# A decoder layer on one core: packing the query weights after the first keys, turning x1 before the cross value halves, and another order in the last section and the scatters

## The chip, the cores and the metric

The kernel runs on one core of a Trainium2 chip. The metric is the device time of one execution in microseconds (us), as the median of several runs. All times below are in us from the start of the span of one profiled execution, unless it is said otherwise. The engines are named as in the profile: PE (TensorE matmul), PEld (its weight load), DVE (VectorE), ACT (ScalarE), POOL (GpSimd) and SP (SyncE, which here issues DMAs). PE's clock can be granted at less than full speed; the profile shows it as a share, 1.00 being full.

## The reference

One decoder layer in float32 over 32 samples of 256 tokens with 256 channels: causal self-attention in a latent space (16 heads, 72 latent channels shared by keys and values), cross-attention to 120 context rows (16 heads of 64), and a mixture of 16 experts in which every expert takes its 32 best tokens of each sample, plus one shared feed-forward. A residual add and a layernorm follow each of the three blocks. Cut to what matters:

```python
kv = x @ latent_w + latent_b                        # (32, 256, 72)
q = einsum('btc,hcl->bhtl', x, Wd_w) + Wd_b         # 16 heads
attn = softmax(causal(q @ kv^T / sqrt(16)))
x1 = layernorm(x + concat_heads(attn @ kv) @ out_w + out_b)

w = softmax((x1 @ Wq * 64**-0.5) @ (ctx @ Wk)^T)    # 16 heads of 64, 120 rows
x2 = layernorm(x1 + (w @ (ctx @ Wv)) @ Wo)

scores = softmax(x2 @ gate_w^T)                     # 16 experts
topk_w, topk_idx = top_k(scores per expert, 32)     # of each sample's 256 tokens
eo = (gelu(xe @ Wg^T) * (xe @ Wu^T)) @ Wd^T * topk_w
out = layernorm(x2 + scatter_add(eo) + shared_expert(x2))
```

## The kernel before

**The rounds.** Attention runs sample by sample. `attention_round(n)` (L778) does the self-attention of sample n, the cross-attention of sample n-1 and the end of the cross-attention of sample n-2 (`cross_out`, `turn_x2`). For n = 1 to 31 the order of PE's instructions is the written one (`manual_schedule` for PE); in round 0 and ahead of it SP's order is the written one too. The other engines' orders are made by a scheduler; what stands in `urgent()` gets a higher priority there. A round takes about 75.5 us. In seven rounds (n = 6, 10, ... 30) the gate's work of four earlier samples is done besides (`routed(n)`, which calls `route` and `score`).

**The first part of a round.** `first_section(n)` (L742) ends with `latent_out(n-1)` (L486): po, the add with x (the r1 add, L496, DVE) and layernorm 1, which makes x1. `layernorm` (L141 to L161) takes its statistics on DVE (L149, L150), rstd on POOL (L152), and the result on DVE again (L154). Then `first_section_rest(n)` (L760) follows with `cross_out(n-2)` (L615: po, the r2 add L625, layernorm 2), `cross_values` (L521: pvx, one half of the heads per call, copied out by ACT), `turn_x1` (L500: transposes into px1T, which `transposed` at L163 has DVE copy into x1T, L172), the second half of `cross_values`, and `cross_queries` (pqx), which reads x1T. `cross_scores` (L555) computes pL and its softmax; POOL does the division, xsm_x (L417). `cross_turn` (L576) transposes that (pxT), `cross_weigh` (L593) applies it to the values (pc). Self-attention has the same steps: `scores` (pS, sm), `turn` (pT), `weigh` (L446, pz), `weigh_rest` (L469, pzr).

**The start.** The block at L838 loads x and the weights, turns x (`turn_x` L297: pxT, xT; POOL then adds out_b, `outb`, to x), computes the keys (`keys` L304: pk) and then queries. `first_weights` (L221) issues the loads of the query weights and packs them from their staging tile ow_sb into wd_sb: two copies at L242 and pack 0 at L236 on DVE, packs 1 to 3 on POOL, and the scalings of wdbs on DVE.

**The last section and the experts.** After round 31 stand `first_section(32)` and a block in which PE's and POOL's orders are both the written ones. There the rest of sample 31's cross-attention alternates with the feed-forward work: `feed_forward()` (L998) is a generator that yields between small stretches of work, and `fill(k)` advances it by k stretches. Its units are (twice) 16 experts and 8 shared ones, each of two samples. An expert's `load` (from L880) has SP load three weight matrices and POOL gather four blocks of 128 rows (xe, L889); `turn` transposes them (px, L898, into xeT); `gated` makes hT (pg and pu, eight stretches); `down` (L910) makes pd in two halves (one stretch each), scales them into a tile eo, and after both scatters four blocks back into acc (L929). The first two stretches are unit 0's `load`, and unit 1's `load` with unit 0's `turn`.

Of the kernel before, what the change touches and what calls it, by code (L numbers as in the profile page):

```python
# [20 lines left out]
F32 = mybir.dt.float32  # L21
# [5 lines left out]
P = 128  # L27
# [5 lines left out]
def decoder_kernel(  # L33
# [140 lines left out]
    def project(acc, pairs):  # L174

        n = len(pairs)
        for i, (lhsT, rhs) in enumerate(pairs):
            nc.tensor.matmul(acc, lhsT, rhs, start=(i == 0), stop=(i == n - 1))  # L178
# [42 lines left out]
    def first_weights():  # L221


        raw = ow_sb.rearrange("p a b -> p (a b)").rearrange("p (c n) -> p c n", c=DC)
        nc.sync.dma_start(out=lat_sb, in_=latent_w.rearrange("(c p) l -> p c l", p=P))
        nc.sync.dma_start(out=raw, in_=wd_w.rearrange("(c p) n -> p c n", p=P))
        nc.scalar.dma_start(out=latb, in_=latent_b.unsqueeze(1))
        nc.scalar.dma_start(
            out=wdbs[:, ZC - 1 : ZC], in_=wd_b[LM:, :].rearrange("l h -> (l h)").unsqueeze(1)
        )  # L230
        nc.scalar.dma_start(out=wdb_sb, in_=wd_b)
        by_head = raw.rearrange("p c (h l) -> p c h l", l=L)

        def pack(copy, g):
            at = slice(2 * g * P, 2 * (g + 1) * P)
            copy(  # L236
                wd_sb[:, :, at].rearrange("p c (h l) -> p c h l", l=LM),
                by_head[:, :, g * HG : (g + 1) * HG, 0:LM],
            )

        for d in range(DC):
            nc.vector.tensor_copy(  # L242
                wd_sb[:, d, H * LM :].rearrange("p (l h) -> p l h", h=H),
                by_head[:, d, :, LM:].rearrange("p h l -> p l h"),
            )

        nc.vector.tensor_scalar(
            wdbs[:, ZC - 1 : ZC], wdbs[:, ZC - 1 : ZC], QSCALE, None, ALU.mult
        )
        pack(nc.vector.tensor_copy, 0)  # L250
        for odd in range(2):
            nc.vector.tensor_scalar(
                wdbs[odd * LM : (odd + 1) * LM, 0 : H // 2],
                wdb_sb[0:LM, :].rearrange("l (c two) -> l c two", two=2)[:, :, odd],
                QSCALE,
                None,
                ALU.mult,
            )
        for g in range(1, NG):
            pack(nc.gpsimd.tensor_copy, g)  # L260
        nc.sync.dma_start(out=outb, in_=out_b.partition_broadcast(P))

    def load_weights(pairs):
        for t, w in pairs:
# [39 lines left out]
    def keys(s):  # L304

        st = states[s]
        pk = bank("r", [L, T], f"pk_{st['nm']}")
        project(pk, [(lat_sb[:, c, :], st["xT"][:, c, :]) for c in range(DC)])
        st["kT"] = sp.tile([L, T], F32, tag="kT", name=f"kT_{st['nm']}")
        with urgent():  # L310
            nc.scalar.activation(st["kT"], pk, AF.Identity, bias=latb)
# [420 lines left out]
    def run(step, s, *args):  # L732
        if 0 <= s < B:
            step(s, *args)
# [7 lines left out]
    def first_section(n):  # L742
# [14 lines left out]
        run(cross_weigh, n - 2, 4)  # L757
        run(latent_out, n - 1)

    def first_section_rest(n):  # L760
        if n:
            run(load, n + 1)
            run(load_context, n + 1)
        run(cross_out, n - 2)
        run(cross_values, n - 1, 0)
        run(turn_x1, n - 1)
        run(cross_values, n - 1, 1)
        if routed(n):
            score((n - 3) // BQ)
        run(cross_queries, n - 1, 0, 0)  # L770
        run(cross_queries, n - 1, 0, 2)
        run(cross_queries, n - 1, 4, 0)
        run(cross_scores, n - 1, 0, 0)
        run(cross_queries, n - 1, 4, 2)
# [63 lines left out]
    with tc.manual_schedule(engines={mybir.EngineType.PE, mybir.EngineType.SP}):  # L838
        load(0)
        first_weights()  # L840
        load_context(0)
        turn_x(0)
        keys(0)
        query_rest(0)
        queries(0, 0)
        values(0)
        load(1)
        load_context(1)
        load_weights([(wk_sb, wk)])
        attention_round(0)  # L850
    with tc.manual_schedule(engines={mybir.EngineType.PE}):
        for n in range(1, B):
            attention_round(n)
        first_section(B)
    self_pools.close()


# [9 lines left out]
    class Expert:  # L867
# [39 lines left out]
        def begin(self):  # L907
            pass

        def down(self):  # L910
            eo = fp.tile([P, NBK, C], F32, tag="eo", bufs=2, name=f"eo_{self.nm}")
            for k0 in range(0, NBK, 2):
                pd = bank("r", [P, 2, C], f"pd_{self.nm}_{k0}")
                for k in range(2):
                    tok = slice((k0 + k) * P, (k0 + k + 1) * P)
                    project(
                        pd[:, k, :], [(self.hT[:, j, tok], self.wd[:, j, :]) for j in range(FC)]
                    )
                for k in range(2):
                    score = self.xe[:, k0 + k, C + self.e : C + self.e + 1]  # L920
                    if k % 2:
                        nc.scalar.activation(eo[:, k0 + k, :], pd[:, k, :], AF.Copy, scale=score)
                    else:
                        nc.vector.tensor_scalar(  # L924
                            eo[:, k0 + k, :], pd[:, k, :], score, None, ALU.mult
                        )
                yield
            for k, b in enumerate(self.blocks):
                nc.gpsimd.indirect_dma_start(  # L929
                    out=acc[b],  # L930
                    out_offset=self.rows(b),
                    in_=eo[:, k, :],
                    in_offset=None,
                    compute_op=ALU.add,
                )

    class Shared:
# [24 lines left out]
                nc.sync.dma_start(out=back, in_=rows.rearrange("(t p) d -> p t d", p=P))  # L962
                self.backs.append(back)

        def down(self):
            for i, back in enumerate(self.backs):
                s = 2 * self.pair + i
                po = bank("r", [P, TC, C], f"pfo_{s}")
                for t in range(TC):
                    tok = slice(i * T + t * P, i * T + (t + 1) * P)  # L970
                    project(
                        po[:, t, :], [(self.hT[:, j, tok], self.wd[:, j, :]) for j in range(FC)]
                    )
                rows = out[s].rearrange("(t p) d -> p t d", p=P)
                parts = [slice(0, TC)] if s < B - 1 else [slice(t, t + 1) for t in range(TC)]
                for part in parts:
                    half = back[:, part, :]
                    nc.vector.tensor_tensor(half, po[:, part, :], half, ALU.add)
                    layernorm(fp, half, half, f"3_{s}_{part.start}")
                    nc.sync.dma_start(out=rows[:, part, :], in_=half)  # L980
                yield

    def gated(unit):

# [13 lines left out]
    def feed_forward():  # L998

        units = []  # L1000
        for part in range(B // HB):
            units += [Expert(part, e) for e in range(E)]
            units += [Shared(pair) for pair in range(part * HB // 2, (part + 1) * HB // 2)]
        units[0].load()
        yield
        units[1].load()
        units[0].turn()
        yield
        for u, unit in enumerate(units):
            unit.begin()  # L1010
            yield from gated(unit)
            if u + 1 < len(units):
                units[u + 1].turn()
            yield from unit.down()
            if u + 2 < len(units):
                units[u + 2].load()


    work = feed_forward()
# [5 lines left out]
    last = B - 1  # L1025
    with tc.manual_schedule(engines={mybir.EngineType.PE, mybir.EngineType.Pool}):
        fill(1)
        first_section_rest(B)
        cross_scores(last, 0, 1)
        turn_x2(last - 1)  # L1030
        fill(2)
        for odd in range(2):
            cross_turn(last, 0, 0, odd)
        fill(1)
        cross_scores(last, 4, 0)
        for odd in range(2):
            cross_turn(last, 0, 1, odd)
        fill(2)
        cross_weigh(last, 0)
        cross_scores(last, 4, 1)  # L1040
        for odd in range(2):
            cross_turn(last, 4, 0, odd)
        fill(4)
        for odd in range(2):
            cross_turn(last, 4, 1, odd)
        fill(1)
        cross_weigh(last, 4)
        fill(1)
        cross_out(last)
        fill(3)  # L1050
        turn_x2(last)
        fill(1)
        route(last // BQ)
        fill(1)
        score(last // BQ)
        fill(3)
        select(B // BG - 1)
        fill(8)
        place(B // BG - 1)
        for _ in work:  # L1060
            pass
# [52 lines left out]
```

## Time and profile before

| what | us |
|---|---|
| median of 3 runs | 3493.84 (3493.35 to 3494.77) |
| the profiled execution | 3492.36 |
| its span (first to last instruction) | 3490.2 |
| mean granted PE clock in the span | 0.997 |
| a round without routing, with routing | 75.5, 76.4 |
| one expert unit, once attention is over | 21.5 |

The first rows of the table differ in what they measure: the span leaves out 2.2 us that lie around the instructions, and the profiled execution is one run of its own, 1.5 us below the median. Times that are worked out from the trace belong to the profiled execution.

In the lists below, a line of the timeline gives start, busy time, engine, source line, operation, output and inputs with their shapes, and the count of instructions grouped; in brackets stands the idle time ahead of it and what released it. The time of a group of matmuls includes the modelled drain of its last one, so the next group may start before the end that is shown.

### The profile page before, as it was taken

What the parts mean: (1) busy time and instruction counts of PE and PEld (TensorE: products, weight loads), DVE (VectorE), ACT (ScalarE), POOL (GpSimd) and SP (SyncE); (2) the same over time, 40 slices, a digit from 0 to 9 for tenths busy, and PEclk for the clock granted to TensorE, in tenths of its full rate; (3) what the DMA queues carried; (4) which work ended last, traced back from release to release, by engine and by line L of the source; (5) the groups of instructions that cost most, each with busy time, mean ns of one, the idle gap of its engine ahead of it and who ended that gap; (6) DMA issues with size and microseconds to landing.
All of it is one profiled execution on the core that took longest, in us unless ns stands there. A gap on an engine that the chain in (4) does not pass through costs nothing.

```text
span 3490.2 us, 58138 instructions
## 1 busy us (share of the span) xinstructions
PE 3449.6 (99%) x21468; PEld 2617.0 (75%) x21468; DVE 1632.7 (47%) x3639; ACT 1499.0 (43%) x5456; POOL 1090.3 (31%) x1073
## 2 busy tenths in 40 slices
PE   8999999999999999999999999999999999999999
PEld 6888888888888888888888888887666655666655
DVE  4555555556555555654555565554311233221133
ACT  3555544555554455554455565444311111111111
POOL 2333322233322233332223333222344411444410
PEclk9999999999999999999999999999999999999999
DMA  3000000000000000000000000002455532455421
GB/s 96 14 19 17 17 17 21 22 20 16 17 17 20 24 17 20 17 17 16 20 24 20 17 17 17 16 21 71 95 123 125 138 99 61 110 124 127 104 82 51
DMA packets 144561, 164.42 MB, mean 47 GB/s; under 512 B 31384, under 2 KB 120216, under 8 KB 144280
## 3 DMA queue, kind: packets, MB, share of 16 engines
q1 hardware_dynamic: 119392, 126.09, 12.1%
q0 software_dynamic: 24576, 34.62, 5.7%
q8 instruction: 171, 2.80, 0.3%
q14 instruction: 110, 0.90, 0.1%
q10 hardware_dynamic: 312, 0.01, 0.0%
HBM read 105.61 MB, written 50.86 MB: 45 GB/s over the span
## 4 chain that ended last, share of the span: by engine, by line
PE 94%; DVE 3%; issue 1%; POOL 1%; DMA 1%; SPq 0%; ACT 0%; POOLq 0%; DVEq 0%; ACTq 0%
PE po L178 13%; PE pS L390 10%; PE pq L178 7%; PE pqx L178 7%; PE pd L178 6%; PE pg L178 6%; PE pu L178 6%; PE pz L455 5%; PE pT L435 5%; PE pL L562 4%; PE pxT L585 3%; PE pc L601 3%; PE pkx L178 3%; PE pu_s L178 3%; PE pg_s L178 3%; PE pfo L178 3%
## 5 line engine op out<-in xcount | busy, mean ns | idle before, releaser
L417 POOL TENSOR_TENSOR sm<-sm,rs 128x512 f32<-128x512 f32 x384 | 397.0, 1041 | 361.9 <-DVE rs L416 349.9
L417 POOL TENSOR_TENSOR xsm_x<-xsm_x,rs_x 128x480 f32<-128x480 f32 x256 | 252.7, 987 | 708.9 <-DVE rs_x L416 706.2
L409 ACT ACTIVATE sm<-sm,nmax 128x128 f32<-128x128 f32 (+1 forms) x1024 | 461.4, 466 | 18.4 <-DVE nmax L403 16.8
L409 ACT ACTIVATE xsm_x<-pL,nmax_x 128x120 f32<-128x120 f32 x1024 | 360.5, 376 | 124.7 <-DVE nmax_x L572 124.6
L390 PE MATMUL pS<-kT,qT 72*128 72x128 f32 (+1 forms) x2048 | 380.4, 329 | 3.3 <-DMA qT<-q 2.3
L152 POOL TENSOR_TENSOR rstd<-rstd,mhalf 128x2 f32<-128x2 f32 (+1 forms) x97 | 67.2, 693 | 935.4 <-DVE rstd L151 935.4
L390 PEld LDWEIGHTS pS<-kT,qT 72*128 72x128 f32 x2048 | 294.9, 192 | 21.1 <-ACT sm L409 2.6
L929 POOL DMA_INDIRECT acc<-eo,offs x128 | 201.5, 1574 | 324.5 <-DVE eo L924 295.0
L399 DVE TENSOR_TENSOR sm<-pS,mask 128x512 f32<-128x512 f32 x384 | 261.3, 681 | 70.8 <-PE pS L390 65.0
L178 PE MATMUL pq<-xT,wd_sb 128*128 128x256 f32 x1152 | 278.1, 382 | 0.0
L531 ACT COPY vx<-pvx 120x512 f32<-120x512 f32 x64 | 37.5, 586 | 557.2 <-PE pvx L178 557.2
L403 DVE TENSOR_REDUCE nmax<-sm 128x2 f32<-128x512 f32 (+1 forms) x384 | 258.5, 673 | 2.4
L178 PE MATMUL po<-ow_sb,zT 128*128 128x256 f32 x1152 | 257.2, 382 | 0.0
L995 DVE TENSOR_TENSOR hT<-gl,pu 128x512 f32<-128x512 f32 x128 | 87.9, 688 | 342.6 <-PE pu L178 258.8
L178 PEld LDWEIGHTS po<-ow_sb,zT 128*128 128x128 f32 x1152 | 216.2, 190 | 40.2 <-DVE cxT L613 8.8
L178 PE MATMUL pqx<-x1T,wq_sb 128*128 128x256 f32 x1024 | 238.0, 385 | 6.6 <-DVE x1T L172 6.3
L178 PE MATMUL pg<-xeT,wg 128*128 128x512 f32 x512 | 240.8, 593 | 0.8 <-DVE xeT L905 0.8
L178 PE MATMUL pu<-xeT,wu 128*128 128x512 f32 x512 | 240.6, 592 | 0.0
L178 PEld LDWEIGHTS pqx<-x1T,wq_sb 128*128 128x128 f32 x1024 | 189.4, 190 | 55.6 <-DVE x1T L172 28.3
L178 PEld LDWEIGHTS pq<-xT,wd_sb 128*128 128x128 f32 x1152 | 210.4, 191 | 25.4 <-issue 0.2
L178 PE MATMUL pd<-wd,hT 128*128 128x256 f32 x1024 | 226.6, 379 | 0.0
L178 PE MATMUL po<-wo_sb,cxT 128*128 128x256 f32 x1024 | 226.2, 379 | 0.0
(130 smaller groups left out, 5833.9 us busy)
## 6 DMA issues: line engine op xcount, KB each, us to landing
wg<-in_wg_dram SPq DMA_DIRECT2D x32, 512.0 KB
wu<-in_wu_dram SPq DMA_DIRECT2D x32, 512.0 KB
wd<-in_wd_dram SPq DMA_DIRECT2D x32, 512.0 KB
x<-in_x_dram SPq DMA_DIRECT2D x32, 256.0 KB
qT<-q SPq DMA_DIRECT2D x512, 8.0 KB
rows<-x SPq DMA_DIRECT2D x32, 256.0 KB
acc<-x SPq DMA_DIRECT2D x32, 256.0 KB
x2t<-x2T SPq DMA_DIRECT2D x32, 256.0 KB
```

What stands on the lines that cost most here:

```text
L178: nc.tensor.matmul(acc, lhsT, rhs, start=(i == 0), stop=(i == n - 1))
L390: nc.tensor.matmul(pS[:, a, :], st["qT", g][:, j, t * P : (t + 1) * P], st["kT"][:, 0:width], start=True, stop=True,)
L399: nc.vector.tensor_tensor(sm, pS, m.unsqueeze(1).to_broadcast([P, n, width]), ALU.add)
L403: nc.vector.tensor_reduce(nmax, sm, AX.X, ALU.max, negate=True)
L409: nc.scalar.activation(dst[:, a, :], src[:, a, :], AF.Exp, bias=nmax[:, a : a + 1], accum_out=rs[:, a, :],)
L417: nc.gpsimd.tensor_tensor(dst, dst, rs.to_broadcast([P, n, width]), ALU.mult)
L435: nc.tensor.transpose(pT[:, j, :], block, ident)
L455: nc.tensor.matmul(pz[odd * LM : (odd + 1) * LM, a, k * P :], st["v"][:, k, 0:LM], moving(st, g, 2 * a + odd, k), start=(k == 0), stop=(k ...
L562: nc.tensor.matmul(pLs[odd][:, j, :], st["qxT", c0][rows, j, t * P : (t + 1) * P], st["kxT"][rows, c0 + j, :], start=True, stop=True,)
L585: nc.tensor.transpose(pT[:, j, :], st["xsm", c0, t, odd][:, j, :], ident)
L601: nc.tensor.matmul(pc[odd * DH : (odd + 1) * DH, a, :], st["vx"][:, 2 * (c0 + j0 + a) + odd, :], st["xpt", c0, odd][:, j0 + a, :], start=True,
L929: nc.gpsimd.indirect_dma_start(out=acc[b], out_offset=self.rows(b), in_=eo[:, k, :], in_offset=None, compute_op=ALU.add,)
```

## The change

Four edits.

1. `first_weights` keeps the loads (that of outb among them); the packing goes into a new function `order_weights`, which is called after `keys(0)`.
2. In `first_section_rest`, `turn_x1(n-1)` now stands ahead of both calls of `cross_values`; for n = 1 one half stays where it was.
3. `first_section(32)` is replaced by `last_section()`: the two last weighs of sample 31 are set around its turns, the two cross turns of sample 30 go behind `latent_out`, and sample 30's `cross_weigh` goes to the next block, behind the first `fill(1)`. In that block `turn_x2(30)` and one stretch of feed-forward (the one with unit 1's `load` and unit 0's `turn`) go ahead of `cross_scores(31, 0, 1)`.
4. `down` takes the half as an argument. Each half has its own tile eo (four buffers of half the size instead of two), and scatters its two blocks at once. The `load` of the unit after next is in the same stretch as the second half, ahead of its yield; it was behind it.

```diff
@@ first_weights
         nc.scalar.dma_start(out=wdb_sb, in_=wd_b)
+        nc.sync.dma_start(out=outb, in_=out_b.partition_broadcast(P))
+
+    def order_weights():
+        raw = ow_sb.rearrange("p a b -> p (a b)").rearrange("p (c n) -> p c n", c=DC)
         by_head = raw.rearrange("p c (h l) -> p c h l", l=L)
...
         for g in range(1, NG):
             pack(nc.gpsimd.tensor_copy, g)
-        nc.sync.dma_start(out=outb, in_=out_b.partition_broadcast(P))
@@ the sections
+    def last_section():
+
+        weigh(B - 1, 2)
+        for b in range(3):
+            turn(B - 1, 3, b)
+        weigh(B - 1, 3)
+        weigh_rest(B - 1)
+        latent_out(B - 1)
+        for odd in range(2):
+            cross_turn(B - 2, 4, 1, odd)
+
     def first_section_rest(n):
         if n:
             run(load, n + 1)
             run(load_context, n + 1)
+        if n == 1:
+            cross_values(0, 0)
         run(cross_out, n - 2)
-        run(cross_values, n - 1, 0)
         run(turn_x1, n - 1)
+        if n > 1:
+            run(cross_values, n - 1, 0)
         run(cross_values, n - 1, 1)
@@ the start, and after the rounds
         keys(0)
+        order_weights()
         query_rest(0)
...
-        first_section(B)
+        last_section()
@@ Expert
-        def down(self):
-            eo = fp.tile([P, NBK, C], F32, tag="eo", bufs=2, name=f"eo_{self.nm}")
-            for k0 in range(0, NBK, 2):
...
-                yield
-            for k, b in enumerate(self.blocks):
+        def down(self, k0):
+
+            k0 *= 2
+            eo = fp.tile([P, 2, C], F32, tag="eo", bufs=4, name=f"eo_{self.nm}_{k0}")
...
+            for k in range(2):
+                b = self.blocks[k0 + k]
                 nc.gpsimd.indirect_dma_start(
                     out=acc[b],
@@ feed_forward
-            yield from unit.down()
+            unit.down(0)
+            yield
+            unit.down(1)
             if u + 2 < len(units):
                 units[u + 2].load()
+            yield
@@ the last block
         fill(1)
+        cross_weigh(last - 1, 4)
         first_section_rest(B)
+        turn_x2(last - 1)
+        fill(1)
         cross_scores(last, 0, 1)
-        turn_x2(last - 1)
-        fill(2)
+        fill(1)
```

`Shared.down` is split by samples in the same way.

More of the change, by code (lines that the diff above doesn't have):

```diff
@@ L908, in begin @@
             pass
-        def down(self):
-            eo = fp.tile([P, NBK, C], F32, tag="eo", bufs=2, name=f"eo_{self.nm}")
-            for k0 in range(0, NBK, 2):
[L913 to L926, printed above, removed]
-                yield
-            for k, b in enumerate(self.blocks):
+        def down(self, k0):
+            k0 *= 2
+            eo = fp.tile([P, 2, C], F32, tag="eo", bufs=4, name=f"eo_{self.nm}_{k0}")
+            pd = bank("r", [P, 2, C], f"pd_{self.nm}_{k0}")
+            for k in range(2):
+                tok = slice((k0 + k) * P, (k0 + k + 1) * P)
+                project(pd[:, k, :], [(self.hT[:, j, tok], self.wd[:, j, :]) for j in range(FC)])
+            for k in range(2):
+                score = self.xe[:, k0 + k, C + self.e : C + self.e + 1]
+                if k % 2:
+                    nc.scalar.activation(eo[:, k, :], pd[:, k, :], AF.Copy, scale=score)
+                else:
+                    nc.vector.tensor_scalar(eo[:, k, :], pd[:, k, :], score, None, ALU.mult)
+            for k in range(2):
+                b = self.blocks[k0 + k]
                 nc.gpsimd.indirect_dma_start(
@@ L963, in begin, with down @@
                 self.backs.append(back)
[L965 to L981, printed above, removed]
+        def down(self, i):
+            s = 2 * self.pair + i
+            back = self.backs[i]
+            po = bank("r", [P, TC, C], f"pfo_{s}")
+            for t in range(TC):
+                tok = slice(i * T + t * P, i * T + (t + 1) * P)
+                project(po[:, t, :], [(self.hT[:, j, tok], self.wd[:, j, :]) for j in range(FC)])
+            rows = out[s].rearrange("(t p) d -> p t d", p=P)
+            parts = [slice(0, TC)] if s < B - 1 else [slice(t, t + 1) for t in range(TC)]
+            for part in parts:
+                half = back[:, part, :]
+                nc.vector.tensor_tensor(half, po[:, part, :], half, ALU.add)
+                layernorm(fp, half, half, f"3_{s}_{part.start}")
+                nc.sync.dma_start(out=rows[:, part, :], in_=half)
     def gated(unit):
```

## The prediction

> **What bounds the kernel.** I read four views, from coarse to fine. First the page: busy time, and the chain that ended last.
>
> ```profile
> span 3490.2 us, 58138 instructions
> PE 3449.6 (99%) x21468; PEld 2617.0 (75%) x21468; DVE 1632.7 (47%) x3639; ACT 1499.0 (43%) x5456; POOL 1090.3 (31%) x1073
> PE 94%; DVE 3%; issue 1%; POOL 1%; DMA 1%; SPq 0%; ACT 0%; POOLq 0%; DVEq 0%; ACTq 0%
> ```
>
> TensorE is the bound nearly everywhere. The change adds and removes no matmul, so it can only take from the 40.6 us in which PE is idle (3490.2 - 3449.6), from small delays between matmuls that count as busy, and from stretches at half clock. Second view: what PE waits for.
>
> ```profile
> PE pk L178 <- DVE xT L172: 7.4, 1, 7.4
> PE pqx L178 <- DVE x1T L172: 6.3, 24, 0.3
> PE pxT L585 <- POOL xsm_x L417: 4.2, 2, 2.3
> PE px L898 <- DMA xe<-rows,offs: 2.9, 2, 2.6
> ```
>
> Columns: total us, times, longest. Each part of the change aims at one row. The third view is the timeline around each wait; the fourth is the order of instructions on each engine in the two built programs, laid side by side.
>
> **Part 1, the query weights: 0.** In the words the packing goes behind keys(0); in the built program only GpSimd's order changes (x+outb, 1.41 us, goes between packs 1 and 2). On DVE nothing moves:
>
> ```profile
> 10.57 0.84 DVE L236 COPY wd_sb<-ow_sb 128x512 f32<-128x512 f32 x1
> 11.77 0.68 DVE L172 COPY xT<-pxT 128x512 f32<-128x512 f32 x1
> ```
>
> The pack still stands ahead of the xT copy that ends PE's 7.4 us wait. Packs 2 and 3 come 1.4 us later; the first matmul that reads pack 2 runs at 33.98, long after. The outb load is queued where it was. If the copy had moved, pk (1.7) and about 1.1 of copy and hand-over would leave the path: 2.9.
>
> **Part 2, x1T before both value halves: 14.3.** A stalled round, then one that does not stall (n=1, where this order stays):
>
> ```profile
> 2123.05 0.60 PE L168 MATMUL px1T<-ident,x 128*128 128x128 f32 x4
> 2123.48 1.88 PE L178 MATMUL pvx<-wv_sb,c 128*120 128x512 f32 x4
> 2125.62 5.45 PE L178 MATMUL pqx<-x1T,wq_sb 128*128 128x256 f32 x24 [0.26 <-DVE x1T L172]
> 2131.00 1.16 PE L562 MATMUL pL<-kxT,qxT 64*128 64x120 f32 x16
> ...
> 79.33 1.88 PE L178 MATMUL pvx<-wv_sb,c 128*120 128x512 f32 x4
> 81.04 5.34 PE L178 MATMUL pqx<-x1T,wq_sb 128*128 128x256 f32 x24
> 86.32 1.16 PE L562 MATMUL pL<-kxT,qxT 64*128 64x120 f32 x16
> ...
> 2124.89 0.68 DVE L172 COPY x1T<-px1T 128x512 f32<-128x512 f32 x1
> ```
>
> From pvx to pL the first takes 7.52, the second 6.99. The 0.26 shown is only half of it: starts tell 0.53. The x1T copy ran at 2124.89 because it stood behind layernorm 2 on DVE. Now px1T starts at 2121.33, 3.4 us (two value halves) ahead of pqx, and the copy stands directly behind the r2 add (2121.53 + 0.69), ahead of layernorm 2: it would end near 2122.9, 2.3 us before pqx at 2125.20. What it delays is layernorm 2 by 0.68, read by turn_x2 15 us later. n = 2 to 31 are 30 rounds, 23 like this and 7 with routing, where the gate's two transposes stand in the wait already (they take 0.42 from 2277.11 instead of 0.22; that 0.20 and the 0.10 after it are to win, 0.30): 23 x 0.53 + 7 x 0.30 = 14.3. The cover is x1: done at 2118.07 (DVE's timeline), wanted at 2121.33, slack 3.3.
>
> **Part 3a, last_section: 6.9.** Before, PE ran out of work behind GpSimd's normalisation of xsm_x, and its clock fell:
>
> ```profile
> 2397.28 1.11 PE L585 MATMUL pxT<-ident,xsm_x 128*120 128x128 f32 x4 [2.31 <-POOL xsm_x L417]
> 2400.32 1.11 PE L585 MATMUL pxT<-ident,xsm_x 128*120 128x128 f32 x4 [1.93 <-POOL xsm_x L417]
> 2401.36 3.76 PE L455 MATMUL pz<-pt,v 128*64 128x256 f32 x32
> ...
> 2396.00:2398.00 2.00, 0.72 (x4) 0.70 (x4) 0.16 (x1) 1.32 (x8) 0.99 (x1) 0.62 0.00 0
> 2398.00:2400.00 2.00, 0.39 (x2) 0.00 (x0) 0.78 (x2) 0.00 (x0) 0.72 (x1) 0.50 0.03 8
> ```
>
> (Window columns: us, busy PE, PEld, DVE, ACT, POOL, granted clock, DMA share, GB/s.) I laid the new order against the old ready times: weigh(31,2) to 2393.06; the turns wait for sm to 2394.10 and end 2394.75; weigh(31,3) waits 0.55 and 0.4 for the pt copies, ends 2397.1; the rest weigh 2399.84; latent_out 2407.71 (before 2417.54); the two cross turns 2408.58; cross_weigh waits 0.72 for its xpt copy, now behind the r1 add on DVE; pqx starts 2421.97 against 2428.79, pL 2427.25 against 2434.16. Counted the other way: five waits gone, 5.4 (0.26 + 0.34 + 0.56 + 2.31 + 1.93), with 0.16 each for the drain of the last matmul that a group's time includes (four pvx show 1.88, yet start every 1.72): 0.8. Clock: eight transposes took 2.1 where eight take 0.86, weigh's 32 matmuls 3.7 where the same take 2.76: 2.2. pqx's wait 0.5, new waits -1.9. Sum 7.0. Nothing of this is late for a queue: on GpSimd xe_0's four gathers (all ahead of it now) end about 2414.6, x1 is ready 2416.2, px1T wants it 2418.1. Their rows landed within 7 us before and px wants them 20 us later. On SP two of the shared expert's weight loads pass sample 30's stores; both are read much later.
>
> **Part 3b, turns before cross_scores(31,0,1): about 0.** px2T and px (1.36) fill the wait in front of pL_0_1, which brings the gain to 9.3 at pg_0_0 (2433.2 for 2442.46). But fill(1) also issues unit 1's gathers, and GpSimd's order is as written:
>
> ```profile
> 2445.58 1.03 POOL L889 DMA_INDIRECT xe<-rows,offs  x1 [0.16 <-issue]
> 2449.43 0.95 POOL L889 DMA_INDIRECT xe<-rows,offs  x1 [0.30 <-issue]
> ```
>
> Four take 4.8 us with their gaps. They stood behind xsm_0_1's normalisation; now they run ahead of it, 2434.7 to 2439.6. pxT_0_1 would want its input at 2438.6 and gets it at 2440.6: a stall of 2.0 + 0.55, so pg_0_1 starts 2442.1 (2448.98 before), gain 6.9. **The Trainium skill** ("TensorE: Matmul & The Clock Gate", Part 1, architectural detail) says GpSimd is strict FIFO: moved-up gathers are paid in full by whatever stands behind them; counting only the filled wait one would write 9.3. The same page (HAM oscillation) asks for no PE gap above some 3.4 us; by that this stall, and the 2.3 of before, costs no clock. The rows differ: with gaps of 2.31 and 1.93 the clock stood at 0.50 (6.8 us at half speed, 2396.45 to 2403.28). So the new stall may cost clock, up to half a 6.8 us stretch: +3.4 at one end, 0 at the other. I take 0: two gaps of 2.3 and 1.9 stood there, here one; a gap of 2.63 near the end of part 4's stretch kept full clock (below). It is close.
>
> **Part 4, halves of down: 3.4.** Before, unit 0's scatters stood on GpSimd behind an rstd released at 2483.08, and unit 2's gathers behind the scatters:
>
> ```profile
> 2495.53 0.95 POOL L889 DMA_INDIRECT xe<-rows,offs  x1 [0.30 <-issue]
> ...
> 2500.33 0.77 PE L898 MATMUL px<-ident,xe 128*128 128x128 f32 x5 [2.63 <-DMA xe<-rows,offs]
> ...
> 2497.00:2499.00 2.00, 0.42 (x2) 0.14 (x1) 0.96 (x2) 0.00 (x0) 0.00 (x0) 1.00 0.97 241
> ```
>
> px_2 to pd took 4.23 (2496.71 to 2500.94); eight such transposes without a wait take 0.87: 3.36 goes. Now the scatters start about 2469 and the gathers end about 2483.5; that rstd runs about 0.6 later, and turn_x2(31) has 0.8 left. The window shows the clock at 1.00 in spite of the gap. Later units are PE-bound (21.5 us each by the distance of their first pg); their scatters were issued slice by slice already: 0.
>
> **Sum**: 0 + 14.3 + 6.9 + 0 + 3.4 = 24.6, minus 3492.36 of the profiled run = 3467.8. The median shown lies 1.5 above that run, so **3469**.
>
> **Rivals.** (a) The new POOL stall brings half clock: 3472.5. For it: the 2.3 us wait of before; against: the 2.63. (b) Better: the xT copy does come early (2.9), or the stall is hidden: 3466 or less. For it: the words of the change; against: DVE's order. (c) The rounds' 0.53 is lost again later in each round: gain 10.3, 3483.4. Against: PE has no other wait in the rounds. (d) Nothing in all: 3493. (e) Slower: x1 itself late. px1T is now in front of 3.4 us of matmuls that used to cover x1. If x1 came d later than in this trace, each of 30 rounds would lose d - 3.3; it outweighs the 24.6 from d = 4.1 on, and at d = 4.4 gives 3469 + 30 x 1.1 = 3502. For it: latent_out's r1 add, statistics and rstd pass DVE, GpSimd and DVE again, and each could meet other work; against: nothing in the change puts anything in front of them in a round, and GpSimd had been idle for 13.6 us before that rstd.
>
> **How the numbers follow.** Forecast 50% (its own range 3466 to 3471.5), (a) 31%, (b) 8%, (c) 6%, (d) 3%, (e) 2%. The range 3464 to 3476 takes in (a) and most of (b). 0.2% is 7.0 us, about what a measurement can tell: faster 0.95 (all but d and e), same 0.03, slower 0.02.
>
> **What would show it.** Right: the pqx row gone, pvx-pL 7.0 in a round; no pxT wait at 2397, full clock there; px_2 about 0.9; pk's wait still 7.4; a new wait of about 2 us of pxT for xsm_x near 2439. Wrong: px1T waiting for DVE x in the rounds, a clock of 0.5 behind the new stall, or pk starting before 12.

## The result and the profile after

The changed kernel takes 3466.60 us (median of 6 runs, 3463.73 to 3468.61); the kernel before, in its runs on the same chip, 3494.11 (3491.12 to 3495.50). The ratio is 0.9921, with a 95% interval of 0.9908 to 0.9934: 27.5 us less, where the forecast was 24.6 less. The profiled execution took 3463.73 and is the fastest of the six. From the first part of its page, and the shares of its chain that ended last:

```profile
span 3461.9 us, 58143 instructions
PE 3435.6 (99%) x21468; PEld 2615.1 (76%) x21468; DVE 1629.3 (47%) x3639; ACT 1497.2 (43%) x5456; POOL 1088.7 (31%) x1073
PE 98%; ACT 0%; DMA 0%; DVE 0%; POOL 0%; SPq 0%; issue 0%; POOLq 0%; ACTq 0%
```

PE has the same 21468 matmuls, is busy 14.0 us less (no half clock, and fewer of the small delays that count as busy), and is idle 26.3 us in place of 40.6. Of the waits of PE (total, times, longest), two rows that the forecast spoke of are left:

```profile
PE pk L178 <- DVE xT L172: 6.9, 1, 6.9
...
PE pxT L588 <- POOL xsm_x L420: 1.8, 2, 1.6
```

The row of pqx waiting for x1T is gone, and so is that of px waiting for its gathers. The 1.8 of pxT is a new wait at a new place. Line numbers have moved a little: L420 is what L417 was. Names with numbers below: xsm_0_1 and pxT_0_1 belong to `cross_scores(31, 0, 1)`, pg_0_1 is unit 0's second pg, px_2 is unit 2's px, px2T is the tile that `turn_x2` writes, and pkx are the keys of the context.

A round of the changed kernel in PE's timeline (start, busy, then the operation; in brackets a wait):

```profile
2105.25 0.60 PE L168 MATMUL px1T<-ident,x 128*128 128x128 f32 x4
2105.68 3.60 PE L178 MATMUL pvx<-wv_sb,c 128*120 128x512 f32 x8
2109.12 5.34 PE L178 MATMUL pqx<-x1T,wq_sb 128*128 128x256 f32 x24
2114.39 1.16 PE L565 MATMUL pL<-kxT,qxT 64*128 64x120 f32 x16
```

and the same time on DVE:

```profile
2105.45 0.69 DVE L628 TENSOR_TENSOR r<-po,x 128x512 f32<-128x512 f32 x1 [3.46 <-PE po L178]
2106.06 0.68 DVE L172 COPY x1T<-px1T 128x512 f32<-128x512 f32 x1
2106.65 0.74 DVE L149 BATCH_NORM_STATS2 st<-r 128x6 f32<-128x256 f32 x2
```

The copy now stands between the r2 add and the statistics of layernorm 2, ends at 2106.74, and pqx wants it 2.4 us later. The half of pvx ahead of pqx, with pqx, takes 2107.40 (its start is half of 3.44 behind 2105.68) to 2114.39, 6.99: the figure of the round that never stalled.

The end of the last section, on PE and then on POOL:

```profile
2422.65 0.65 PE L588 MATMUL pxT<-ident,xsm_x 128*120 128x128 f32 x4 [1.56 <-POOL xsm_x L420]
2423.58 0.65 PE L588 MATMUL pxT<-ident,xsm_x 128*120 128x128 f32 x4 [0.28 <-POOL xsm_x L420]
2424.07 1.88 PE L178 MATMUL pg<-xeT,wg 128*128 128x512 f32 x4
```

```profile
2416.77 1.03 POOL L907 DMA_INDIRECT xe<-rows,offs  x1 [0.16 <-issue]
...
2420.63 0.95 POOL L907 DMA_INDIRECT xe<-rows,offs  x1 [0.30 <-issue]
2421.60 1.93 POOL L420 TENSOR_TENSOR xsm_x<-xsm_x,rs_x 128x480 f32<-128x480 f32 x2
```

The division of xsm_0_1 starts the moment the fourth gather ends, and PE waits for it. The clock stayed at 1.00 here. Last, unit 2's turn on PE, without the wait of before:

```profile
2471.81 1.04 PE L916 MATMUL px<-ident,xe 128*128 128x128 f32 x8
2472.68 7.07 PE L178 MATMUL pd<-wd,hT 128*128 128x256 f32 x32
2479.59 1.88 PE L178 MATMUL pg<-xeT,wg 128*128 128x512 f32 x4
```

The reason stands on POOL, first in the kernel before, then in the changed one: the scatters (acc) now run ahead of the rstd, and the gather instructions behind them end 13.2 us ahead of px_2.

```profile
2483.08 0.72 POOL L152 TENSOR_TENSOR rstd<-rstd,mhalf 128x2 f32<-128x2 f32 x1 [19.99 <-DVE rstd L151]
2484.00 1.78 POOL L929 DMA_INDIRECT acc<-eo,offs  x1 [0.20 <-issue]
...
2444.53 1.64 POOL L944 DMA_INDIRECT acc<-eo,offs  x1 [6.84 <-DVE eo L941]
...
2457.62 0.95 POOL L907 DMA_INDIRECT xe<-rows,offs  x1 [0.30 <-issue]
2458.59 0.73 POOL L152 TENSOR_TENSOR rstd<-rstd,mhalf 128x2 f32<-128x2 f32 x1
```

Cut at the same instructions, the two profiled executions compare like this (us; starts on PE):

| stretch | before | after | gain | forecast |
|---|---|---|---|---|
| start to round 0's first pkx | 35.95 | 31.84 | 4.1 | 0 |
| to the last pkx of round 31 | 2353.95 | 2340.09 | 13.9 | 14.3 |
| to pg_0_1 in the last block | 59.08 | 52.14 | 6.9 | 6.9 |
| to px_2 | 47.73 | 47.74 | 0 | 0 |
| to the first pg of unit 2 | 11.13 | 7.78 | 3.35 | 3.4 |
| to the end | 982.36 | 982.31 | 0 | 0 |

In the stretches where the forecast placed its steps, they came close to what was computed. Two questions are left: what the 4.1 at the start are, where part 1 moved nothing on PE, DVE, ACT or SP; and why the medians differ by 27.5 where the steps give 24.

### The profile page after: what moved, and what is told of

Read it like the earlier page. It is cut to its first block, busy times and chain, and to the rows that moved or that the text cites. A ratio compares the mean times of both kernels' runs of the same rounds, so it can differ in the third digit from the quotient of the medians.

```text
span 3461.9 us, 58143 instructions
## 1 busy us (share of the span) xinstructions
PE 3435.6 (99%) x21468; PEld 2615.1 (76%) x21468; DVE 1629.3 (47%) x3639; ACT 1497.2 (43%) x5456; POOL 1088.7 (31%) x1073
## 4 chain that ended last, share of the span: by engine, by line
PE 98%; ACT 0%; DMA 0%; DVE 0%; POOL 0%; SPq 0%; issue 0%; POOLq 0%; ACTq 0%
PE po L178 14%; PE pS L393 10%; PE pq L178 7%; PE pqx L178 7%; PE pd L178 6%; PE pg L178 6%; PE pu L178 6%; PE pz L458 5%; PE pT L438 5%; PE pL L565 4%; PE pc L604 3%; PE pxT L588 3%; PE pkx L178 3%; PE pu_s L178 3%; PE pg_s L178 3%; PE pvx L178 3%
## 5 line engine op out<-in xcount | busy, mean ns | idle before, releaser
L420 POOL TENSOR_TENSOR sm<-sm,rs 128x512 f32<-128x512 f32 x384 | 396.6, 1040 | 359.0 <-DVE rs L419 338.2
L420 POOL TENSOR_TENSOR xsm_x<-xsm_x,rs_x 128x480 f32<-128x480 f32 x256 | 252.4, 986 | 676.6 <-DVE rs_x L419 672.5
L412 ACT ACTIVATION_READ_ACCUMULATOR xsm_x<-pL,nmax_x 128x1 f32 x1024 | 225.6, 220 | 0.0
```

The costliest lines, as they stand in the source:

```text
L412: nc.scalar.activation(dst[:, a, :], src[:, a, :], AF.Exp, bias=nmax[:, a : a + 1], accum_out=rs[:, a, :],)
L420: nc.gpsimd.tensor_tensor(dst, dst, rs.to_broadcast([P, n, width]), ALU.mult)
```

## The experiments

**Each part alone, and the changed kernel again.** Each of three kernels is the kernel before with one part of the diff above; their edits are those hunks, unchanged: part 2 the one in `first_section_rest`, part 3 `last_section` and the last block, part 4 `down` and `feed_forward`. The changed kernel itself ran once more. Later kernels ran in other sets, in part on other chips, each with the kernel before beside them; a gain in its own set is one against those runs.

> The changed kernel once more, for its clock. Its runs so far fall in two groups, 3463.7 to 3464.4 us with clock 1.000 and 3466.0 to 3468.6 with 0.998. Theory: the slower ones have one stretch of 6.8 us at half clock right behind GpSimd's new stall near 2421 us (the forecast's rival a), at a cost of some 3 us. Rival: the stretch lies behind the wait for the query DMA in round 0, near 26 us, where the kernel before has one too. The median should again be 3464 to 3468.

> The kernel before with part 2 alone (x1T before both value halves). Theory: 30 rounds and the last section gain together 14.3 + 0.5 = 14.8 us, so about 3479.3; the row of pqx waiting for x1T is gone and a round's pvx to pL takes 7.0. Rival: the 0.53 is lost again later in each round and the gain is 4 or less (3490).

> The kernel before with part 3 alone (last section and the order of the turns). Theory: 6.9 less the 0.5 of pqx's wait, which stays: 6.4, about 3487.7; the half clock stretch at 2396 to 2403 us is gone, and pxT waits some 1.8 us for POOL xsm_x behind unit 1's gathers. Rival: the new stall brings the half clock back, and the gain is 3 (3491).

> The kernel before with part 4 alone (scatters by halves, load before the yield). Theory: px_2 no longer waits for its gathers, 3.4 us, about 3490.7; px_2 to pd takes 0.9 us. Rival: the rstd of the last cross_out now stands behind scatters and gathers on POOL and px2T or the route waits for x2 instead: 0 to 2.

| kernel | median, us | runs | less than before (3493.12, 34 runs) |
|---|---|---|---|
| changed, again | 3465.94 (3464.15 to 3467.51) | 5 | 27.2 |
| part 2 | 3479.19 (3478.80 to 3481.16) | 5 | 13.9 |
| part 3 | 3486.92 (3484.01 to 3489.17) | 14 | 6.2 |
| part 4 | 3488.34 (3486.01 to 3490.69) | 21 | 4.8 |

Parts 2 and 3 alone are close to what was expected of each (14.8 and 6.4). Part 4 is more than the 3.36 of its wait. As to the clock, the windows of the changed kernel's second profile (us, busy PE, PEld, DVE, ACT, POOL, granted clock, DMA share, GB/s) decide for the rival:

```profile
22.00:24.00 2.00, 2.00 (x7) 1.55 (x6) 1.94 (x3) 0.65 (x3) 0.00 (x0) 0.52 0.87 209
...
28.00:30.00 2.00, 0.85 (x3) 0.30 (x2) 0.70 (x2) 1.60 (x5) 0.00 (x0) 0.77 0.25 56
```

The half clock lies in round 0, from 22.0 to 28.9. In windows over the whole span there is only one stretch more, behind 3462, where PE has no work left. Round 0's first pkx starts at 35.63 there, 3.8 later than in the first profile, which has no half clock in its windows until PE's work ends; from there to the last pkx it takes 2340.02 us, the same as in the first (2340.09). Of the 14 profiles kept, 12 have such a stretch in round 0; the changed kernel's first one and that of scatters together (below) have none.

Against the profile of before, 3.3 of the 4.1 lie from the pS that waits for the query DMA (26.87 and 26.10) to pkx, where the kernel before has its half clock. Against the changed kernel's second profile the 3.8 is made up otherwise: 0.6 is a later start of pk, 1.5 are the first twelve pq, and 1.7 lies behind them. The pq in the first profile, then in the second:

```profile
13.81 3.33 PE L178 MATMUL pq<-xT,wd_sb 128*128 128x256 f32 x12
16.98 0.29 PE L321 MATMUL pv<-ident,kT 72*128 72x72 f32 x2
...
14.44 4.85 PE L178 MATMUL pq<-xT,wd_sb 128*128 128x256 f32 x12
19.12 0.29 PE L321 MATMUL pv<-ident,kT 72*128 72x72 f32 x2
```

The profile shows the granted clock as 1.00 there in both, though the median pq of these twelve takes 634 ns in the second profile, where the median over all pq of the first is 379. Why the pace of these twelve differs is open.

**Two parts together.** The three single gains sum to 24.9, the whole gained 27.2. The 95% intervals of the single gains are 4.5 to 10 us wide, so this difference is not clear of noise.

> The kernel before with parts 3 and 4. Single gains were 13.9 (part 2), 6.2 (part 3) and 4.8 (part 4), sum 24.9; the whole gained 27.2. Theory: the 2.3 are half clock stretches that the kernels with one part still have behind px_2's or pxT_0_1's wait and the whole kernel mostly has not; parts 3 and 4 together then gain more than 11.0, some 13, about 3480.5, and no half clock stands behind 2440. Rival: the parts add up, 11.0, about 3482.5, and the 2.3 are scatter between sets of runs.

> The kernel before with parts 2 and 3; px_2's wait for its gathers stays. Theory: 20.1 as the sum of both, about 3473.4, so that part 4 is worth 6 to 7 on top of it where its wait itself is 3.4: the rest is half clock behind that wait, which the trace shows in some stretch after 2470. Rival: 3470, part 4 on top is worth the 3.4 of its wait.

Parts 3 and 4 took 3482.23 (3480.92 to 3484.22, 7 runs), 10.5 below the kernel before (3492.74); parts 2 and 3 took 3471.20 (3469.38 to 3474.09, 5 runs), 21.5 below. The first pair adds up (6.2 + 4.8 = 11.0), against the theory. The second lies between the two forecasts: part 3 on top of part 2 is worth 7.6, and part 4 on top of both 5.2 (3471.20 - 3466.00, the median of the changed kernel's 11 runs), or 5.7 to 6.0 if each is compared with the kernel before in its own set. As to the cause, the traces bear out the theory. With parts 2 and 3, unit 2's turn still waits, and what follows is slow:

```profile
2478.00 0.77 PE L912 MATMUL px<-ident,xe 128*128 128x128 f32 x5 [2.92 <-DMA xe<-rows,offs]
2478.60 8.76 PE L178 MATMUL pd<-wd,hT 128*128 128x256 f32 x32
2487.20 1.88 PE L178 MATMUL pg<-xeT,wg 128*128 128x512 f32 x4
```

The 32 pd take 8.60 from start to start, 6.91 in the changed kernel. The clock in the windows there was 0.75, 0.50 and 0.89. I measured the stretch from px_2 to the next pg in every profile that has this wait; 7.78 is its length without:

| profile | px_2 to pg | lost |
|---|---|---|
| before | 11.13 | 3.35 |
| part 2 | 12.39 | 4.61 |
| part 3 | 12.58 | 4.80 |
| parts 2 and 3 | 13.00 | 5.22 |
| layernorm 2 behind the turn (below) | 13.95 | 6.17 |

The mean is 4.8; part 4 alone gained as much. The profile of before that I forecast from is the only one of the five in which no half clock followed the wait. And with parts 3 and 4 the half clock did follow the new wait of pxT_0_1 (PE's timeline, then the windows):

```profile
2441.57 1.11 PE L585 MATMUL pxT<-ident,xsm_x 128*120 128x128 f32 x4 [0.28 <-POOL xsm_x L417]
2442.47 3.13 PE L178 MATMUL pg<-xeT,wg 128*128 128x512 f32 x4
```

```profile
2442.00:2444.00 2.00, 2.00 (x6) 1.15 (x5) 0.58 (x2) 1.73 (x8) 0.00 (x0) 0.50 0.00 0
2444.00:2446.00 2.00, 2.00 (x5) 0.85 (x4) 0.18 (x1) 1.98 (x11) 0.99 (x1) 0.76 0.00 0
```

From that pxT on to the next pu it takes 3.87 (2441.57 to 2445.44), 2.21 in the changed kernel (2423.58 to 2425.79): 1.7 for the clock. The profile of part 3 alone shows the same (1.5; this execution, 3489.17, was the slowest of its 14); the profiles of kernels that hold parts 2 and 3 both (two of the changed kernel, and those without part 1, with xT first, with scatters together, with parts 2 and 3) do not, in six of six. That fits part 3 being worth more on top of part 2. Why the same wait brought the half clock in the one group and not in the other, or whether that is chance, is not settled.

**Part 1.** One kernel is the changed one with the packing back in `first_weights`:

```diff
-        order_weights()
```

> The changed kernel without part 1 (the packing back in first_weights, the outb load behind it). Theory: part 1 moves nothing that PE waits for, so the time is that of the changed kernel within 1 us, 3465 to 3467. Rival: the three parts alone gained 13.9, 6.2 and 4.8, in sum 24.9, where the whole change gained 27.2; the 2.3 left over are part 1's (x+outb earlier on GpSimd, or the order of the loads), and this run comes to 3468 or more.

It took 3467.04 (3466.84 to 3467.81, 5 runs), 1.04 above the changed kernel's 3466.00, between what theory and rival said; against the kernel before in its own set (3494.45) it gains 27.4, as the changed kernel did (27.5 and 27.2). So no worth of part 1 shows that is clear of noise. Its first pkx starts at 35.22. One thing stays open: all eight profiles of kernels without part 1 have the half clock in round 0, and two of the four with it and the same order on DVE do not. That is too few to say whether part 1 makes the stretch rarer. The other kernel does what the words of the change say, by giving DVE a written order in the head of the start block too:

```diff
-    with tc.manual_schedule(engines={mybir.EngineType.PE, mybir.EngineType.SP}):
+    head = {mybir.EngineType.PE, mybir.EngineType.SP}
+    with tc.manual_schedule(engines=head | {mybir.EngineType.DVE}):
         load(0)
...
         order_weights()
+    with tc.manual_schedule(engines=head):
         query_rest(0)
```

> The changed kernel with DVE's order at the start made the written one, so that the xT copy stands in front of the packing, as the words of the change say. Theory: pk starts near 6 us and pq at 10.2 to 11.3, when DVE's packing ends, in place of 13.8 to 14.4: 2.9 us less, about 3463. Rival: the gain is used up at the waits that follow in round 0 (qT's copies, the DMA of q), or the half clock stretch of round 0 moves with it: 0 to 1.

It took 3462.59 (3460.78 to 3465.87, 5 runs), 3.4 below the changed kernel; against the kernel before in its own set it gains 31.9, 4.4 to 4.7 more than the changed kernel did in its sets. Its timeline on PE, and the copy on DVE:

```profile
5.88 1.98 PE L178 MATMUL pk<-xT,lat_sb 128*72 128x256 f32 x4 [0.78 <-DVE xT L172]
10.02 4.24 PE L178 MATMUL pq<-xT,wd_sb 128*128 128x256 f32 x12 [2.16 <-DVE wd_sb L246]
```

```profile
5.13 0.69 DVE L172 COPY xT<-pxT 128x512 f32<-128x512 f32 x1 [2.71 <-PE pxT L168]
```

pk now stands at 5.88 and waits 0.78; the wait that ends last is pq's, for the packed weights, whose copy starts at 9.69, when their load has landed. pq starts at 10.02 where the changed kernel's two profiles have it at 13.81 and 14.44, and the first pkx at 31.83 against 35.00 to 35.95 in the eight other profiles with DVE's order as before whose half clock in round 0 is as long (6.8 us).

**Layernorm 2 behind the turn.** This is to tell the two causes apart that part 2 could have: px1T's place on PE, or the copy's place on DVE. The kernel before, with `cross_out` split:

```diff
-        run(cross_out, n - 2)
+        run(cross_out, n - 2, False)
         run(cross_values, n - 1, 0)
         run(turn_x1, n - 1)
+        run(cross_norm, n - 2)
```

> The kernel before; only cross_out's layernorm 2 is written behind turn_x1. PE's order is that of the kernel before, px1T between the value halves. On DVE the x1T copy goes up by one place: between the two halves of layernorm 2's result (L154) in place of behind both, some 0.36 us earlier. Theory: the copy's place behind layernorm 2 is what pqx waited for; each of the 23 rounds gains about 0.36 and pqx's row is nearly gone: 8 to 10 in all, about 3484. Rival: it is px1T's place on PE that decides, and nothing changes (3493).

It took 3483.41 (3480.94 to 3485.64, 7 runs), 10.4 less than the kernel before in its set (3493.82). DVE in a round, then PE:

```profile
2115.36 0.41 DVE L154 TENSOR_SCALAR x<-r,mv,rstd 128x256 f32<-128x256 f32 x1 [0.81 <-POOL rstd L152]
2115.69 0.68 DVE L172 COPY x1T<-px1T 128x512 f32<-128x512 f32 x1
2116.29 0.40 DVE L154 TENSOR_SCALAR x<-r,mv,rstd 128x256 f32<-128x256 f32 x1
```

```profile
2114.61 1.88 PE L178 MATMUL pvx<-wv_sb,c 128*120 128x512 f32 x4
2116.43 5.45 PE L178 MATMUL pqx<-x1T,wq_sb 128*128 128x256 f32 x24
2121.80 1.16 PE L562 MATMUL pL<-kxT,qxT 64*128 64x120 f32 x16
```

One place up on DVE, with PE's order as before, takes pqx's wait away: pvx to pL is 7.19, between the 7.52 of before and the 6.99 of the changed kernel. From round 0's first pkx to the last one of round 31 (35.00 to 2379.76) this profile takes 2344.76, 9.2 less than before. So the copy's place in DVE's queue alone, with px1T where it was, brings 9.2 of the 13.9; the copy still ends only 0.06 ahead of pqx. Part 2 moves the copy further up, by moving px1T, and brings the rest.

**Unit 1's gathers behind the scores.** The changed kernel with its stretch split, so that POOL divides xsm_0_1 first:

```diff
         units[0].load()
         yield
+        units[0].turn()
+        yield
         units[1].load()
-        units[0].turn()
         yield
...
         cross_scores(last, 0, 1)
-        fill(1)
+        fill(2)
```

> The changed kernel with unit 1's gathers behind cross_scores(31,0,1) on GpSimd, so behind xsm_0_1's division; PE's order is the same. Theory: xsm_0_1 is ready near 2420.5, pxT_0_1 does not wait (1.56 + 0.28 with their restarts, 2.2 in all), about 3463.8. Rival: DVE and ACT deliver the sums for xsm_0_1 too late anyway, and the wait only changes its releaser: 0 to 0.5.

The trace does what was expected (PE, then POOL):

```profile
2421.98 1.16 PE L565 MATMUL pL<-kxT,qxT 64*128 64x120 f32 x16
2423.07 1.09 PE L588 MATMUL pxT<-ident,xsm_x 128*120 128x128 f32 x8
2423.99 1.88 PE L178 MATMUL pg<-xeT,wg 128*128 128x512 f32 x4
```

```profile
2421.85 0.98 POOL L420 TENSOR_TENSOR xsm_x<-xsm_x,rs_x 128x480 f32<-128x480 f32 x1 [0.87 <-DVE rs_x L419]
2422.99 1.03 POOL L907 DMA_INDIRECT xe<-rows,offs  x1 [0.16 <-issue]
```

pxT_0_1 does not wait, and from px1T (2402.41; 2400.37 in the changed kernel) to pg_0_1 it takes 21.58 in place of 23.70: 2.1. Of that the median, 3465.43 (3463.98 to 3466.27, 5 runs), shows 0.6, or 1.5 to 1.8 if each kernel is compared with the kernel before in its own set; runs that lie 2 to 5 us apart do not resolve it.

> The last two together. Theory: they are at different places and add up, 2.9 + 2.2 = 5.1 us below the changed kernel, about 3461, and 32 below the kernel before. Rival: 1 to 3 below.

The kernel with both edits took 3461.59 (3460.28 to 3464.40, 4 runs), 4.4 below the changed kernel's 3466.00, of 5.1 expected, and 32.9 below the kernel before in its set, where 32 was expected; the ratio to the kernel before is 0.9909 (0.9894 to 0.9925). It has the lowest median of all that ran.

**Scatters together.** The changed kernel, with the four scatters of an expert written behind the second half:

```diff
-            for k in range(2):
-                b = self.blocks[k0 + k]
+            self.eos = [eo] if k0 == 0 else self.eos + [eo]
+            for k, b in enumerate(self.blocks if k0 else ()):
...
-                    in_=eo[:, k, :],
+                    in_=self.eos[k // 2][:, k % 2, :],
```

> The changed kernel with an expert's four scatters together behind the second half, still ahead of the yield and of the next load. Theory: it is the place ahead of the yield that took away px_2's wait, and that stays away. But the first scatter starts at 2450.0 in place of 2444.5, so gathers and the rstd of the last cross_out behind them come 3.7 later; px2T has 1.0 of slack there and waits 2.7, with its restart 2.8 in all: about 3469. Rival: halves matter for nothing, the time is that of the changed kernel, 3466.

It took 3467.35 (3463.67 to 3468.02, 5 runs), the changed kernel's time, and px2T does not wait. My expectation was wrong before it ran: nothing else stands between the halves in POOL's queue, so its order is the same in both texts, and the first scatter still leaves as soon as its half of eo is done. The time is the rival's, but for that reason this run does not test the halves: each half still has its own tile and its own moment. What the traces show is that px_2's wait went away where scatters and gathers stand ahead of the last cross_out's rstd in that queue (with part 4 alone the first scatter starts at 2469.57 and the rstd at 2483.66). How much of that the split tiles are needed for stays untested.

## Why the prediction was right

**Part 1, forecast 0: right,** as far as the runs resolve it (3467.04 without it, 3466.00 with it), and pk's wait stayed (6.9). The 2.9 named for a copy that does move was 3.4 to 4.7 when it was made to.

**Part 2, forecast 14.3 in the rounds: right.** The trace gives 13.9, the kernel with part 2 alone 13.9. The mechanism, the copy behind layernorm 2, was shown by moving the copy alone, which brought 9.2 of it. The cover that was computed held: from n = 2 on px1T never waits for x1 (the one such wait, 1.6 at n = 1, stands in both profiles).

**Part 3, forecast 6.9: right,** 6.94 in the trace, with the new wait of 1.56 + 0.28 for POOL where 2.0 + 0.55 was computed. That the sum fits to 0.1 is in part luck: at pg_0_0 the gain is 9.1 where 9.3 was computed, and 2.1 of it is given back where 2.4 was, so two small errors cancel. It was right to book the gathers in full: with them behind, 2.1 comes back.

**The clock behind the new wait, taken as 0: right for the changed kernel** in both of its profiles, though the same wait did bring 1.5 and 1.7 in the two kernels that have part 3 without part 2. The rival with 3472.5 fell. But one of the two reasons given did not hold: the gap of 2.63 that kept full clock, px_2's, was followed by half clock in each of the four other profiles with that wait. For this term the forecast was lucky as much as right.

**Part 4, forecast 3.4: mechanism right, size too small.** The term "3.36 goes" was read from the one profile in which the clock stayed full behind the wait. In four of four other profiles with the same wait it did not, and the mean loss over the five is 4.8.

**The sum.** 24.6 was forecast, 27.5 measured. Of the missing 2.9, an estimated 1.4 is the clock in part 4 (4.8 less 3.4, from the five profiles above). It would also explain why the profile of before lies 1.5 below its median; the forecast carried this 1.5 over to the changed kernel, where that wait is gone. For the other 1.5 round 0 is the candidate: the changed kernel's two profiled executions (3463.73 and 3467.51) differ by the 3.8 that lies ahead of pkx, three of its 11 runs have a mean clock of 1.000 (3463.73 to 3464.39), and none of the 34 of the kernel before is above 0.998. As only one profile of the kernel before was kept, this is not shown; the interval of the ratio is 9 us wide in any case. Rival b would nearly have reached this time too, but not by its causes: the copy did not come early, and the stall was not hidden. Rivals c, d and e fell: no round gave its gain back, and x1 was never late.

## What to carry to other kernels

When a wait is short but repeats in each round, compare the starts of two rounds, one with and one without it, in place of the idle time that the profile shows: here 0.53 against 0.26. Look at what stands ahead of the awaited instruction in its own queue; moving one copy ahead of a layernorm that nobody waits for was half of the whole gain, and written order changes nothing on an engine whose queue comes out the same. And take a stall's price from several executions: a PE gap of 2 to 3 us can be followed by half clock that costs 1.3 to 2.8 us more in one execution, and by none in another.

## What the runs showed of the hardware

**Half clock behind short gaps.** The granted clock fell to 0.50 behind gaps of 1.6 to 2.9 us on PE, in some executions and not in others with the same gap: behind px_2's wait in four of five profiles, behind pxT_0_1's in two of eight. Behind the two waits of the old last section, 2.31 and 1.93 with only four transposes between them, it fell in four of four (before, parts 2 and 4 alone, layernorm 2 behind the turn).

**Two lengths.** If the windows are added up (2 us at clock 0.75 count as 1 us at half speed), each of the 22 stretches that lie where PE still had work comes to 3.4 or 6.8 us.

**No single gap length decides.** In round 0 of the changed kernel's second profile the stretch of 6.8 us from 22.0 follows 2 us in which PE was busy 1.40, with no gap above 0.60; in the kernel before the one from 27.6 follows a gap of 2.26; in the changed kernel's first profile and in that of scatters together gaps of 2.44 and 2.55 at this place were followed by full clock. A rule of one length for such gaps does not cover that; the Trainium skill ("TensorE: Matmul & The Clock Gate", Part 1, HAM oscillation) asks for no gap above some 3.4 us, and every gap named here was shorter.
